# Hybrid layer on one core: the first chunk's keys are spread by VectorE out of PSUM, and the first scores follow at once

## The chip, the cores and the metric

The kernel runs on one core of a Trainium2 chip. The metric is the device time of one execution in microseconds (us). Times of engines and transfers come from one execution recorded by the hardware profiler. Engines are called PE (TensorE: matmuls, with PEld for its weight loads), DVE (VectorE), ACT (ScalarE), POOL (GpSimd) and SP (SyncE, which here only issues transfers).

## The reference

Input x is (4, 1024, 128) in float32. Four blocks follow each other, each added to x: a sparse causal attention with 16 heads of 8 channels, a feed-forward net with weights of +1 and -1, a Mamba block, and the same feed-forward net again. The change is in the attention, whose core is:

```python
x = x + attn(_layernorm(x), Wq, Wk, Wv, Wo)
# in attn: T = 1024, H = 16, HEAD_DIM = 8
mask   = causal & ((cols >= rows - 31) | ((rows - cols) % 64 == 0))
scores = einsum('bhqd,bhkd->bhqk', Q, K) * HEAD_DIM ** -0.5
attn   = softmax(where(mask, scores, -inf))
out    = einsum('bhqk,bhkd->bhqd', attn, V)
```

A query sees the 32 keys up to its own place, and every 64th key before.

## The kernel before

**Tiles and chunks.** A tile of the attention holds 64 places of two batch rows, 128 partitions in all. There are 32 tiles; four make a chunk (`cc`, 0 to 7). For each chunk `prep_steps` normalizes x (`xn`), turns it with PE (`tp`, copied by ACT as `xnT`), projects it to turned queries and keys (`pq`, `pk`, each a PSUM bank of 128 x 512) and to rows of queries, keys and values (`pn`, one per tile, from which ACT copies `qs`, `kv`, `vS`). The values also make a way through DRAM: a transfer `vd<-kv` writes them, four transfers `vr<-vd` read them in another order, and ACT spreads each of the four into `vb`.

**Keys.** The scores of near keys come from matmuls with 64 channels (8 heads) on the partitions at once. For that a chunk's keys stand in `kx`, 128 x (4 tiles x 8 x 128): for each partition, which belongs to one head, only the block of its own head holds keys, the other seven blocks are zero. There are two such buffers, `kxs`, cleared once by POOL (`gp.memset`). The keys get there by ACT's copy `kT<-pk` and 16 transfers `kx<-kT`, one per head. For chunk 0 they are dealt to the queues of SP, ACT and POOL, for chunk 1 to SP and POOL, later to SP alone.

**One tile.** `scores` (PE, into `ps`, one PSUM buffer for all tiles) and `keep_scores` (ACT copies the own half of ps to `S`), `scores_before` (DVE adds the masked other half by predicated copies), `softmax_scores` (DVE), `softmax_exp` (ACT, `E`). POOL forms the products for the strided keys (`prod`, `prodv`); PE turns the weights (`pt`), multiplies with `vb` (`pa`), and projects (`po`, `py`).

**Order.** Within the attention every instruction of PE, DVE, ACT and POOL keeps the order in which Python issues it (`InOrder`, whose line 57 therefore stands for nearly all instructions in the profile). Transfers issued by an engine stand in that engine's order too. The loop `for i in range(-LEAD, last + 5)` issues, in turn i, the stages of several tiles; `at(k, stage)` means the stage of tile i + k. A chunk's `prep_steps` is a generator that advances twice per turn; it starts in the turn that `starts` names, which is turn -7 for chunk 0, -6 for chunk 1 and 1 for chunk 2. The scores of tile i + 1 are issued in turn i, so those of tile 0 in turn -1, behind the preparation of chunk 1 so far issued. `spread_values` (ACT, one quarter of a chunk's values per turn) comes at the end of a turn, before the next turn's copy of S.

**The very start.** `tables` makes the identity, masks and small index tables from two POOL iotas (`row`, `col`). Behind it POOL clears kxs[0]; `stats` (DVE) and `scales` (POOL) of the first two chunks give the normalization; then POOL clears kxs[1] and both `vb`.

After the attention the feed-forward and Mamba parts run from queues of pieces whose order is fixed while the program is built.

Of the kernel before, what the change touches and what calls it, by code (L numbers as in the profile page):

```python
# [16 lines left out]
F32 = mybir.dt.float32  # L17
BF16 = mybir.dt.bfloat16
I32 = mybir.dt.int32
# [3 lines left out]
ALU = mybir.AluOpType  # L23
# [3 lines left out]
P = 128  # L27
# [4 lines left out]
H, HD = 16, 8  # L32
# [7 lines left out]
CH = 512  # L40
# [3 lines left out]
def hybrid_kernel(ctx: ExitStack, tc: tile.TileContext, x, Wq, Wk, Wv, Wo, ln_g, ln_b, W_in, conv_w,  # L44
                  conv_b, W_xp, W_dt, b_dt, A_log, D_param, W_out, res_scale, k0, k1, k2, s0, s1, s2, out):
    nc = tc.nc
# [15 lines left out]
    ve, te, sc, gp = (InOrder(e) for e in (nc.vector, nc.tensor, nc.scalar, nc.gpsimd))  # L62
    const = ctx.enter_context(tc.tile_pool(name="const", bufs=1))
# [32 lines left out]
    prev_mask = const.tile([P, W], I32, name="prev_mask")  # L96
    own_t = const.tile([P, W], F32, name="own_t")
    prev_t = const.tile([P, W], F32, name="prev_t")
    k0s = const.tile([P, 2, FF], U8, name="k0s")
    k1s = const.tile([P, 4, FF], U8, name="k1s")  # L100
    k2s = const.tile([P, 4, C], U8, name="k2s")
# [5 lines left out]
        for i, s in enumerate((s0, s1, s2, res_scale)):  # L107
            nc.sync.dma_start(scal[:, i : i + 1], s.partition_broadcast(P))

    def tables():  # L110
        with tc.tile_pool(name="setup", bufs=1) as setup:
            row = setup.tile([P, P], I32, name="row")
            gp.iota(row, pattern=[[0, P]], base=0, channel_multiplier=1)
            col = setup.tile([P, P], I32, name="col")
            gp.iota(col, pattern=[[1, P]], base=0, channel_multiplier=0)

            ve.tensor_tensor(ident, row, col, ALU.is_equal)
            row31 = row
            ve.tensor_single_scalar(row31, row, 31, op=ALU.bitwise_and)

            ve.tensor_tensor(prev_mask, col[:, :W], row31[:, :W], ALU.is_gt)

            ve.tensor_tensor(own_t, col[:, :W], row31[:, :W], ALU.is_ge)
            ve.tensor_tensor(prev_t, row31[:, :W], col[:, :W], ALU.is_gt)
            ve.tensor_copy(spread_ids[:, 0], row31[:, :N])
            ve.tensor_copy(spread_ids[:, 1], col[:, N : 2 * N])
# [64 lines left out]
    def attention(actx):  # L191
# [7 lines left out]
        pw = actx.enter_context(tc.tile_pool(name="attps", bufs=1, space=PSUM))  # L199
        pr = actx.enter_context(tc.tile_pool(name="attpr", bufs=5, space=PSUM))  # L200
        tiles = [(bp, m) for bp in range(NP) for m in range(NT)]
        HB = H // 2

        def spare(name):
            return pr.tile([P, CH], F32, tag="pr", name=name)
# [15 lines left out]
        sc.activation(warm, neg, AF.Exp)  # L221
        load_x(0, range(1, NT // 4), nc.sync)
        load_x(1, range(NT // 4), nc.sync)
        tables()

        def weights_in():
            wt = spare("wt")
# [23 lines left out]
            gp.tensor_scalar_mul(rs[:, 1], mv[:, :, 0], -1.0)  # L251
            gp.tensor_mul(rs[:, 1], rs[:, 1], rs[:, 0])

        gp.memset(kxs[0], 0.0)
        for cc in range(2):
            stats(cc)
            scales(cc)
        gp.memset(kxs[1], 0.0)
        for t in vbs:
            gp.memset(t, 0.0)  # L260
# [6 lines left out]
        prep = {}  # L267

        def prep_steps(cc):

            bp, c = divmod(cc, NT // 4)
            yield
            xn = ap2.tile([P, 4, C], F32, name=f"xn{cc}", tag="xn")
            rs = norms.pop(cc)
            for i in range(4):
                sc.activation(
                    xn[:, i, :], xs[bp][:, 4 * c + i, :], AF.Identity, bias=rs[:, 1, i : i + 1],
                    scale=rs[:, 0, i : i + 1],
                )
            yield  # L280
            tp = spare(f"tp{cc}")
            for i in range(4):
                te.transpose(tp[:, i * P : (i + 1) * P], xn[:, i, :], ident)
            yield
            xnT = ap2.tile([P, CH], F32, name=f"xnT{cc}", tag="xnT")
            sc.copy(xnT, tp)
            yield
            pq, pk = spare(f"pq{cc}"), spare(f"pk{cc}")
            te.matmul(pk, wqkv[:, 1, :], xnT, start=True, stop=True)
            te.matmul(pq, wqkv[:, 0, :], xnT, start=True, stop=True)  # L290

            def project(i):
                pn = spare(f"pn{cc}_{i}")
                te.matmul(
                    pn[:, : 3 * C], xnT[:, i * P : (i + 1) * P], wqkv.rearrange("p i c -> p (i c)"),
                    start=True, stop=True,
                )
                return pn

            qs = ap2.tile([P, 4, C], F32, name=f"qs{cc}", tag="qs")  # L300

            def keep_rows(i, pn):
                m = 4 * c + i
                sc.copy(qs[:, i], pn[:, :C])
                sc.copy(kv[bp][:, m], pn[:, C : 3 * C])
                sc.copy(vS[bp][:, :, m], pn[:, 2 * C : 3 * C])

            yield
            kT = ap2.tile([P, CH], F32, name=f"kT{cc}", tag="kT")
            sc.copy(kT, pk)  # L310
            kx = kxs[cc % 2]
            queues = ((nc.sync, nc.scalar, nc.gpsimd), (nc.sync, nc.gpsimd))[cc] if cc < 2 else (nc.sync,)
            for h in range(H):
                rows = slice(h * HD, (h + 1) * HD)
                queues[h % len(queues)].dma_start(
                    kx[rows, :, h % HB, :], kT[rows, :].rearrange("p (t x) -> p t x", t=4)
                )
            qT = ap2.tile([P, CH], F32, name=f"qT{cc}", tag="qT")
            sc.copy(qT, pq)
            for i0 in (0, 2):  # L320
                yield
                pn = project(i0), project(i0 + 1)
                yield
                keep_rows(i0, pn[0])
                keep_rows(i0 + 1, pn[1])
            vd = dram.tile([4, P, C], F32, name=f"vd{cc}")
            nc.sync.dma_start(vd.rearrange("t p c -> p t c"), kv[bp][:, 4 * c : 4 * c + 4, C:])
            vr = ap2.tile([P, 16, C], F32, name=f"vr{cc}", tag="vr")
            for a in range(4):
                nc.sync.dma_start(  # L330
                    vr[a * W : (a + 1) * W], vd.rearrange("t (g k) c -> k (t g) c", k=W)
                )
            prep[cc] = qT, kx, qs, vr
# [4 lines left out]
        def scores(i):  # L338

            bp, m = tiles[i]  # L340
            qT, kx, _, _ = prep[i // 4]
            q0 = i % 4 * P
            before_tile = prep[(i - 1) // 4][1][:, (i - 1) % 4] if m else None
            ps = psum["s", i] = pw.tile([P, H, 2, W], F32, name=f"ps{i}", tag="ps")
            for g in range(4):
                rows = slice(g * W, (g + 1) * W)
                for hf in range(2):
                    ch = slice(hf * 64, hf * 64 + 64)
                    heads = slice(hf * HB, (hf + 1) * HB)
                    q = qT[ch, q0 + g * W : q0 + (g + 1) * W]  # L350
                    te.matmul(
                        ps[rows, heads, 0, :], q, kx[ch, i % 4, :, g * W : (g + 1) * W], start=True, stop=True
                    )
                    if g % 2:
                        before = kx[ch, i % 4, :, (g - 1) * W : g * W]
                    elif m:
                        before = before_tile[ch, :, (g + 1) * W : (g + 2) * W]
                    else:
                        continue
                    te.matmul(ps[rows, heads, 1, :], q, before, start=True, stop=True)  # L360
            S[i] = ap2.tile([P, H, W + NT - 1], F32, name=f"S{i}", tag="S")

        def keep_scores(i):
            sc.copy(S[i][:, :, :W], psum["s", i][:, :, 0, :])
# [160 lines left out]

        LEAD = 7

        starts = {(cc if cc < 2 else 4 * cc) - LEAD: cc for cc in range(len(tiles) // 4)}
        preps = []
        last = len(tiles)  # L530
        for i in range(-LEAD, last + 5):
            def at(k, stage):
                if 0 <= i + k < last:
                    stage(i + k)

            if i == -LEAD:
                weights_in()
            if i == 0:
                load_mlp()
            at(-1, strided_products)  # L540
            at(1, product)
            at(-2, weights)
            at(0, scores_before)
            at(-4, divide)
            at(-2, strided)
            at(-2, weights_own)
            at(-2, weights_all)
            at(-2, weights_before)
            at(-5, project_out)
            at(-5, residual)  # L550
            at(1, scores)
            at(1, keep_scores)
            at(0, softmax_scores)
            at(0, softmax_exp)
            if i in starts:
                preps.append(prep_steps(starts[i]))
            for p in preps:
                next(p, None)
            at(-4, turn_out)
            at(-3, values)  # L560
            at(-4, keep_out)
            for p in preps:
                next(p, None)
            cc, step = divmod(i + LEAD, 4)
            if cc + 2 < last // 4:
                stats(cc + 2, range(step, step + 1))
                if step == 3:
                    scales(cc + 2)
            cc, step = divmod(i + 1, 4)
            if 0 <= cc < last // 4:  # L570
                spread_values(cc, range(step, step + 1))
# [681 lines left out]
```

## Time and profile before

| what | value |
|---|---|
| median of 3 runs | 932.8 us (928.43 to 935.38) |
| profiled execution, its own time | 934.96 us |
| its span | 933.2 us |
| mean granted PE clock | 0.89 |
| busy: PE, DVE, ACT, POOL | 760.7, 770.1, 589.3, 756.4 us |
| 0 to 27.7 us: busy PE, DVE, ACT, POOL | 16.5, 9.5, 13.2, 23.8 us |
| 60 to 90 us: busy PE, DVE, ACT, POOL | 24.2, 29.7, 20.4, 28.5 us of 30 |

The span is divided into busy time, per engine, and idle time, which the profile puts down to what ended it. A duration is that of one instruction or of a merged row of several (x4); rows can overlap a little, since an instruction begins while the one before it ends. "SPq", "ACTq" rows are transfers being issued, not their landing.

### The profile page before, as it was taken

Reading aid. Unit: us, or ns where it says so; the run is one execution under the profiler, and the core shown is the slowest. Engines: PE = TensorE matmul, PEld = TensorE weight load, DVE = VectorE, ACT = ScalarE, POOL = GpSimd, SP = SyncE. Lnnn points to the kernel's source line nnn. Section 1 sums busy time; section 2 is a strip of 40 time slices with the busy share of each in tenths; the row PEclk is TensorE's granted clock in tenths of the full one; section 3 lists DMA queues with packets and bytes.
Section 4 is the critical chain, followed back from the end, with each engine's and each line's share of the span. In section 5 each row is a group of like instructions: output and inputs, shape, how many; then the busy total and the mean of one; then the engine's idle time right before and its main releaser. Section 6 shows DMA issues by size and latency. Waiting matters only on the chain.

```text
span 933.2 us, 15285 instructions
## 1 busy us (share of the span) xinstructions
PE 760.7 (82%) x5628; PEld 457.0 (49%) x5628; DVE 770.1 (83%) x1026; ACT 589.3 (63%) x1293; POOL 756.4 (81%) x592
## 2 busy tenths in 40 slices
PE   5697758965697969887789889879889979788886
PEld 2355425643466634532347534536445626445556
DVE  4699898999743268988799999899999998999952
ACT  4676527753345578688666887777868764754613
POOL 8589996999533087999988999989989997997921
PEclk9799979997589989997898998989979988779988
DMA  5733123330100012111221121121211221222000
GB/s 131 128 69 70 26 50 68 71 68 2 30 18 1 27 65 69 46 68 47 67 70 45 51 85 47 67 69 46 79 70 46 79 81 46 80 67 80 24 22 12
DMA packets 47762, 53.35 MB, mean 57 GB/s; under 512 B 5032, under 2 KB 38960, under 8 KB 47688
## 3 DMA queue, kind: packets, MB, share of 16 engines
q1 hardware_dynamic: 46160, 51.69, 20.0%
q8 instruction: 44, 0.72, 0.3%
q0 software_dynamic: 768, 0.35, 0.3%
q10 hardware_dynamic: 760, 0.34, 0.2%
q14 instruction: 30, 0.25, 0.1%
HBM read 45.82 MB, written 4.46 MB: 54 GB/s over the span
## 4 chain that ended last, share of the span: by engine, by line
PE 22%; DVE 22%; ACT 13%; POOL 6%; issue 5%; DVEq 0%; POOLq 0%; ACTq 0%
DVE hs L57 14%; ACT da L57 4%; PE pys L57 4%; DVE hc L57 4%; ACT L57 3%; PE pc L57 3%; POOL db L57 3%; PE pga L57 3%; PE pgb L57 2%; POOL hc L57 2%; ACT waste L57 2%; PE pgc L57 1%; PE pmo L57 1%; PE pfob L57 1%; PE pmo_own L57 1%
## 5 line engine op out<-in xcount | busy, mean ns | idle before, releaser
L57 POOL TENSOR_TENSOR db<-du,bs 128x1024 f32<-128x1024 f32 x128 | 304.0, 2376 | 0.6 <-DMA bs<-bd 0.6
L57 ACT ACTIVATE da<-dt,a_t 128x512 f32<-128x512 f32 x256 | 175.5, 687 | 138.7 <-DVE hs L57 137.9
L57 POOL TENSOR_TENSOR hc<-hc,hc 128x512 f32<-128x512 f32 x128 | 163.8, 1281 | 48.5 <-DVE hc L57 48.4
L57 DVE TENSOR_TENSOR hc<-hs,pcc 128x1024 f32<-128x1024 f32 x128 | 155.9, 1218 | 20.3 <-PE pcc L57 12.2
L57 DVE TENSOR_TENSOR_SCAN hs<-da,db 128x512 f32<-128x512 f32 x128 | 149.1, 1206 | 13.7 <-ACT da L57 13.7
L57 DVE TENSOR_TENSOR_SCAN hs<-da,carry,db 128x512 f32<-128x512 f32 x128 | 157.0, 1268 | 1.9 <-ACT da L57 1.0
L57 PE MATMUL pys<-hc,ident 128*128 128x512 f32 x256 | 148.4, 666 | 0.1
L57 PE MATMUL pga<-h1a,w 128*128 128x512 f32 x256 | 76.3, 448 | 10.4 <-ACT u L57 2.9
L57 PE MATMUL pcc<-bc,spread 96*128 96x512 bf16 x128 | 52.1, 407 | 34.7 <-DVE hc L57 33.8
L57 PEld LDWEIGHTS pys<-hc,ident 128*128 128x128 f32 x256 | 52.0, 212 | 49.6 <-issue 24.8
L57 POOL TENSOR_TENSOR prodv<-vS,E 128x128 f32<-128x128 f32 (+14 forms) x30 | 69.5, 2318 | 6.7 <-ACT E L57 6.5
L57 POOL TENSOR_TENSOR prod<-kv,qs 128x128 f32<-128x128 f32 (+14 forms) x30 | 71.2, 2372 | 1.5 <-DVE or L57 1.4
L57 PEld LDWEIGHTS pga<-h1a,w 128*128 128x128 f32 x256 | 51.5, 206 | 34.7 <-issue 5.2
L57 ACT ACT_TABLE_LOAD x48 | 61.6, 1283 | 3.5 <-issue 2.7
L57 PE MATMUL pc<-mxnT,w_conv 128*128 128x512 f32 x128 | 62.1, 611 | 2.1 <-ACT gate L57 2.1
L57 PE MATMUL pgb<-h1b,w 128*128 128x512 f32 x192 | 59.3, 458 | 3.8 <-DVE h1b L57 2.7
L57 ACT ACTIVATE E<-S 128x512 f32<-128x512 f32 (+15 forms) x62 | 26.5, 473 | 52.5 <-DVE S L57 52.3
L57 PE MATMUL ps<-kx,qT 64*32 64x256 f32 x1008 | 46.4, 443 | 9.6 <-DVE S L57 9.4
L57 PE MATMUL py<-woT,oT 128*128 128x128 f32 x64 | 17.7, 362 | 41.1 <-ACT oT L57 40.9
L57 PEld LDWEIGHTS pgb<-h1b,w 128*128 128x128 f32 x192 | 39.2, 206 | 22.1 <-issue 6.4
L57 POOL TENSOR_TENSOR ep<-ep,eo 128x512 f32<-128x512 f32 x32 | 41.1, 1286 | 9.9 <-ACT ep L57 8.7
L57 POOL TENSOR_TENSOR du<-dt,u 128x512 f32<-128x512 f32 x16 | 20.8, 1304 | 27.9 <-ACT dt L57 27.9
(209 smaller groups left out, 1577.6 us busy)
## 6 DMA issues: line engine op xcount, KB each, us to landing
bs<-bd SPq DMA_DIRECT2D x64, 512.0 KB
vr<-vd SPq DMA_DIRECT2D x32, 256.0 KB
vd<-kv SPq DMA_DIRECT2D x8, 256.0 KB
x<-in_L_attn_a_x_dram SPq DMA_DIRECT2D x15, 128.0 KB
kx<-kT SPq DMA_DIRECT2D x110, 16.0 KB
out_dram<-x SPq DMA_DIRECT2D x12, 128.0 KB
taps<-in_L_attn_b_conv_w_dram SPq DMA_DIRECT2D x1, 512.0 KB
k1s<-in_L_ffn_k_dram SPq DMA_DIRECT2D x1, 256.0 KB
```

What stands on the lines that cost most here:

```text
L57: ins = getattr(self.engine, name)(*args, **kwargs)
```

## The change

Three things. First, chunk 0's keys no longer go through `kT` and transfers: four DVE operations, one per tile, multiply the bank `pk` (each key row repeated 8 times) with a small table `head_of`, 128 x 8, which is one where a block belongs to the partition's head and zero elsewhere; they write all of `kx`, so kxs[0] is no longer cleared. qT is copied first. Second, `tables` takes the statistics and scales of the first two chunks into itself, behind the identity and ahead of `head_of` and the other tables. Third, the scores of tile 0 and their copy are issued in turn -4, right behind the turn that spread the keys, and chunk 1's preparation starts in turn -4 instead of -6.

```diff
+    HB = H // 2
+    head_of = const.tile([P, HB], F32, name="head_of")
...
-    def tables():
+    def tables(stats, scales):
...
             ve.tensor_tensor(ident, row, col, ALU.is_equal)
+            for cc in range(2):
+                stats(cc)
+                scales(cc)
+
+            eight = setup.tile([P, HB], I32, name="eight")
+            ve.tensor_single_scalar(eight, row[:, :HB], 3, op=ALU.logical_shift_right)
+            ve.tensor_single_scalar(eight, eight, HB - 1, op=ALU.bitwise_and)
+            ve.tensor_tensor(head_of, eight, col[:, :HB], ALU.is_equal)
             row31 = row
...
-        tables()
...
-        gp.memset(kxs[0], 0.0)
-        for cc in range(2):
-            stats(cc)
-            scales(cc)
+        tables(stats, scales)
         gp.memset(kxs[1], 0.0)
...
             yield
-            kT = ap2.tile([P, CH], F32, name=f"kT{cc}", tag="kT")
-            sc.copy(kT, pk)
             kx = kxs[cc % 2]
-            queues = ((nc.sync, nc.scalar, nc.gpsimd), (nc.sync, nc.gpsimd))[cc] if cc < 2 else (nc.sync,)
-            for h in range(H):
-                rows = slice(h * HD, (h + 1) * HD)
-                queues[h % len(queues)].dma_start(
-                    kx[rows, :, h % HB, :], kT[rows, :].rearrange("p (t x) -> p t x", t=4)
-                )
             qT = ap2.tile([P, CH], F32, name=f"qT{cc}", tag="qT")
-            sc.copy(qT, pq)
+            if cc == 0:
+
+                sc.copy(qT, pq)
+                for t in range(4):
+                    ve.tensor_tensor(
+                        kx[:, t], pk[:, t * P : (t + 1) * P].unsqueeze(1).to_broadcast([P, HB, P]),
+                        head_of.unsqueeze(2).to_broadcast([P, HB, P]), ALU.mult,
+                    )
+            else:
+                kT = ap2.tile([P, CH], F32, name=f"kT{cc}", tag="kT")
+                sc.copy(kT, pk)
+                queues = (nc.sync, nc.gpsimd) if cc == 1 else (nc.sync,)
+                for h in range(H):
...
+                sc.copy(qT, pq)
+            prep[cc] = qT, kx
...
-        starts = {(cc if cc < 2 else 4 * cc) - LEAD: cc for cc in range(len(tiles) // 4)}
+        starts = {(3 if cc == 1 else 4 * cc) - LEAD: cc for cc in range(len(tiles) // 4)}
...
-            at(1, scores)
-            at(1, keep_scores)
+            if i == 3 - LEAD:
+                scores(0)
+                keep_scores(0)
+            if i >= 0:
+                at(1, scores)
+                at(1, keep_scores)
```

On SP the order of the first transfers changes with it: `vd` of chunk 0, then one key transfer of chunk 1, the four `vr` of chunk 0, the other seven key transfers of chunk 1, then `vd` and `vr` of chunk 1. Before, all of chunk 1's keys and both `vd` stood ahead of the `vr`.

More of the change, by code (lines that the diff above doesn't have):

```diff
@@ L201, in attention @@
         tiles = [(bp, m) for bp in range(NP) for m in range(NT)]
-        HB = H // 2
         def spare(name):
@@ L308, in prep_steps @@
             yield
-            kT = ap2.tile([P, CH], F32, name=f"kT{cc}", tag="kT")
-            sc.copy(kT, pk)
             kx = kxs[cc % 2]
-            queues = ((nc.sync, nc.scalar, nc.gpsimd), (nc.sync, nc.gpsimd))[cc] if cc < 2 else (nc.sync,)
-            for h in range(H):
-                rows = slice(h * HD, (h + 1) * HD)
-                queues[h % len(queues)].dma_start(
-                    kx[rows, :, h % HB, :], kT[rows, :].rearrange("p (t x) -> p t x", t=4)
-                )
-            qT = ap2.tile([P, CH], F32, name=f"qT{cc}", tag="qT")
-            sc.copy(qT, pq)
+            qT = ap2.tile([P, CH], F32, name=f"qT{cc}", tag="qT")
+            if cc == 0:
[10 more added lines that the diff above has]
+                for h in range(H):
+                    rows = slice(h * HD, (h + 1) * HD)
+                    queues[h % len(queues)].dma_start(
+                        kx[rows, :, h % HB, :], kT[rows, :].rearrange("p (t x) -> p t x", t=4)
+                    )
+                sc.copy(qT, pq)
+            prep[cc] = qT, kx
             for i0 in (0, 2):
@@ L340, in scores @@
             bp, m = tiles[i]
-            qT, kx, _, _ = prep[i // 4]
+            qT, kx = prep[i // 4][:2]
             q0 = i % 4 * P
```

## The prediction

> **What bounds the start now.** I read the page first (span, slices, groups), then the timeline of the first 36 us, since the change touches nothing later, and last the waits from 40 to 290 us. The page gives the span and the row that prices the new VectorE work.
>
> ```profile
> span 933.2 us, 15285 instructions
> ...
> L57 DVE TENSOR_TENSOR hc<-hs,pcc 128x1024 f32<-128x1024 f32 x128 | 155.9, 1218 | 20.3 <-PE pcc L57 12.2
> ```
>
> The timeline of the start (start, duration, engine, operation; in brackets the idle time before it and what ended it):
>
> ```profile
> 1.32 3.50 POOL L57 MEMSET kx<- 128x4096 f32 x1
> ...
> 1.73 3.18 DVE L57 TENSOR_SCALAR row<-row 128x128 int32<-128x128 int32 x1
> ...
> 5.41 0.29 DVE L57 BATCH_NORM_STATS2 sta<-x 128x6 f32<-128x128 f32 x1
> ...
> 9.18 1.65 ACT L57 ACTIVATE xn<-x,rsa 128x128 f32<-128x128 f32 x4 [2.48 <-POOL rsa L57]
> ...
> 12.03 2.07 PE L57 MATMUL pk<-xnT,wqkv 128*128 128x512 f32 x2 [0.68 <-ACT xnT L57]
> ...
> 19.09 0.59 ACT L57 COPY qT<-pq 128x512 f32<-128x512 f32 x1 [4.37 <-DMA kx<-kT]
> ...
> 22.97 5.82 SPq L315 DMA_DIRECT2D kx<-kT  x8
> 23.73 4.04 PE L57 MATMUL pn<-wqkv,xnT 128*128 128x384 f32 x12
> ...
> 27.70 1.11 PE L57 MATMUL ps<-kx,qT 64*32 64x256 f32 x24
> ...
> 29.55 0.82 DVE L57 COPY_PREDICATED_SCALAR S<-prev_mask,neg 32x512 f32 x1 [17.66 <-ACT S L57]
> ...
> 31.31 7.18 SPq L330 DMA_DIRECT2D vr<-vd  x8
> ...
> 34.68 0.62 ACT L57 COPY vb<-vr 32x512 f32<-32x512 f32 x1 [5.16 <-DMA vr<-vd]
> 35.21 0.58 ACT L57 COPY S<-ps 128x512 f32<-128x512 f32 x1
> ...
> 35.82 0.77 DVE L57 COPY_PREDICATED S<-prev_mask,ps 128x512 f32<-128x512 int32 x1 [1.19 <-ACT S L57]
> ```
>
> Four things are to be seen. VectorE's first table operation stands 3.18 us beside GpSimd's memset of kx and ends with it, and the statistics of x begin only behind it. ScalarE is held 4.37 us issuing key transfers before it may copy qT. The first scores (27.70) begin when TensorE's projections of both chunks end (23.73 + 4.04 = 27.77), so the arrival of the keys was not last there: order was. And tile 1's scores are copied at 35.21 because ScalarE stood 5.16 us in front of vb, waiting for the values' way through DRAM. VectorE, the engine that is nearly full afterwards, stands still for 17.66 us meanwhile. The waits from 40 to 290 us show what follows:
>
> ```profile
> ACT E L57 <- DVE S L57: 52.3, 26, 4.4
> PEld py L57 <- ACT oT L57: 48.3, 29, 4.0
> ```
>
> They are engine for engine, no transfer among them. So the attention behind tile 1 is a loop of engines that keeps its own pace, and what tile 1 gains the end gains. The mark I follow is VectorE's first operation on tile 1, at 35.82. In the built program the order of every engine's instructions from tile 3 on is the same before and after.
>
> **The change, part by part.** *Statistics first, no memset of the first kx.* The memset (3.50 us) and the table work are no longer ahead of the statistics, which now wait for x alone. The trace does not show when x's first quarter landed: at the latest at 4.74, when the weights queued behind it on ScalarE's queue released the first transpose; not before 3.3, when the DMA rates of the slices add up to its 262 KB. I take 4.1, so the statistics begin 1.3 us earlier (0.7 to 2.1). From there to pk's end the operations are those of before: four statistics pairs 1.7, GpSimd's scales 2.0, xn at 7.9, pk from 10.7 to 12.8, pq to 14.5.
>
> *Tables behind the statistics.* Three tiny operations are added (two on `eight`, one for `head_of`); the nearest rows, the copies of spread_ids at 5.25 and 5.33, follow each other at 0.1 us, so 0.3 to 0.5. The second chunk's x was there by 7.0, where its statistics began before; so its statistics end by 8.7, the tables and two pairs of the third chunk by about 10.5, and then VectorE waits for pk (12.8): free, with 2 us of cover. If GpSimd's scales held the tables for their longest operation (1.04 us), that would still be covered.
>
> *Spreading.* Four operations of 128x1024, one input in PSUM and one in SBUF. The row with the same output and the same kinds of input is hc<-hs,pcc, 1.22 us: 4 x 1.22 = 4.9 us, from 12.8 to 17.7. Only the first of them, done at 14.1, is waited for by the first scores; qT is later (pq 14.5, copy 0.59, 15.1). The four and five remaining statistics pairs (2.0 us) fall into the 17.66 us in which VectorE stood still. Without that cover they would cost 4.9.
>
> The row and the rule differ here. GpSimd clears the second kx and both vb from 10.7 on (8.7 and scales of 2.0): 3.5 + 2.0 + 1.0 + 2.0 + 1.0 = 9.5 us, to 20.2, just beside the spreading, and the row at 1.73 shows a VectorE operation standing until such a memset is over. The Trainium skill (SBUF — State Buffer, Who interferes with whom) says that only instructions in a two-port mode, or with two SBUF inputs against a GpSimd instruction that reads, share that lock; the integer operation on SBUF fits the first, a spread with one input in PSUM neither. By the row all four come after 20.2, the first scores at 21.4 instead of 15.1, and all behind them 6.3 us later, a net loss of 1.0; by the rule nothing. I take the rule, as the trace has statistics operations (0.26 us at 11.42) unhindered beside the second memset, though they have a single source.
>
> *Removed.* kT's copy of chunk 0 (0.58), five issues on ScalarE (the 4.37 us), six on SP, five on GpSimd. No data wait goes with them on TensorE, as shown; they free the queues.
>
> *First scores at once, chunk 1 two turns later.* Now the way to 35.82 in the new order. Scores of tile 0 at 15.1; rows of ps give 1.11 for 24 at 27.70 and twice as long in slow places, I take 1.5: 16.6. Then S's copy 0.6 (17.25), and the projections of chunk 0, 1.65 for each two (16.45 in the timeline): 18.3 and 19.9. ScalarE: two tiles' rows 1.3 (to 18.95), xn of chunk 1 1.65 (20.6), two more tiles 1.3 (21.9), xnT 0.6 (22.5). TensorE: pk of chunk 1 2.07 (24.6; 1.13 elsewhere, which would bring 0.9 more). kT 0.6 (25.25). SP now has vd of chunk 0, one key transfer, then the four vr, then the other seven. So vr, whose data left at 21.9 and landed by 24.3, waits behind the one that needs kT: 0.7 us, vr issued at 25.95. From issue to vb's start it was 34.68 - 31.31 = 3.37: 29.3. ScalarE is there at 28.4 (behind pk 1.8 for pq, 4 x 0.34 for two projections, 0.65 for the last copies), so vr decides by 0.9. vb 0.62, S of tile 1 0.6: **VectorE begins tile 1 at 30.55, against 35.82: 5.3 us earlier.**
>
> VectorE's work on tile 0 runs meanwhile: spreading and statistics to 19.7, then 4.7 us (29.55 to 34.2 before): 24.4, and tile 1's scores, which reuse its bank, come at 27.9 by TensorE's order. Slack 3.5 us: the spread could cost 0.9 more each and take nothing.
>
> *Who else comes late.* Queued behind GpSimd's eight key issues, which wait for kT (25.25), is prod of tile 1: 8 x 0.54 = 4.3, so 29.6 to 30.1, in time by a hair; 1 us late would cost at most that. On SP the seven keys go behind vr, by 0.7 to 0.8 each and with waits on vr's landings: last issue about 32, landed by 35.5; tile 4's scores need them at 44.43 - 5.3 = 39.1. Cover 3.6 us. vd and vr of chunk 1 follow, landing from about 38.5; needed at 48.94 - 5.3 = 43.6.
>
> Sum: 5.3 us, 4.7 to 7.0 by the bounds of x's landing and pk. The profiled execution took 934.96 (span 933.2 and 1.8 around it), which becomes 929.7; it lay 2.2 above the median, and on the median 932.8 - 5.3 = **927.5**.
>
> **The rivals.** *Larger gain.* vr lands before ScalarE is there, pk and the scores run at their quick rows: another 0.9 + 0.9 + 0.4, x at 3.3 adds 0.8: 8.3, 924.5, and with a favourable draw of the runs' scatter below 923.5. For it: the quick rows exist; against: vr's 3.37 stood on a nearly empty queue. *Nothing gained.* Either the memsets hold the spreads (the row at 1.73; loss 1.0), or vr shares its engines with the keys issued by GpSimd and takes twice 3.37 to vb: gain 1.9. 931 to 934. For it: that the transfer engines were 0.80 busy from 27.7 to 36 us already. *Slower.* The key transfers on SP behind vr run one after the other, each waiting for the landing of one before, at 3.4 us: seven give 24 from 29.5, so 53 at tile 4's scores. It decides once the last key lands after 44.4, the place of those scores before; at 53 it would be 8.6 us slower, 941.4. Against it: eight such transfers took 5.82 at 22.97, 0.73 each.
>
> **How the numbers follow.** Forecast 0.64, larger gain 0.14, nothing gained 0.17, slower 0.05. The three runs of before spread from 928.43 to 935.38, so a median of after can be 3 off by scatter alone. The range goes from 922 (the larger gain with some scatter) to 933.5 (most of nothing gained). Some 1%, 9.3 us, is about what a measurement of this kernel can tell from no change; faster than 923.5 are half of the larger gains and a little of the forecast's scatter, 0.10; slower than 942.1 half of the last and a trace, 0.03; within, 0.87.
>
> **What would show it.** In the profile of after: statistics from about 4.1; four spreads of 1.2 us at 12.8; ps at 15; VectorE's first predicated copies of tile 0 near 20; vb's wait on vr ending at 29.3; tile 1 on VectorE at 30.5, and ps of tile 4 not waiting for keys; further on the same rows 5 us earlier. It would be wrong if a spread takes 2 us or more, if kT of chunk 1 comes after 26, or if a wait on kx stands before tile 4.

## The result, and the profile after

Twelve executions of each kernel, taken side by side, gave a median of 928.91 us after (924.76 to 930.8) against 932.62 before (928.12 to 935.38): the ratio is 0.9962, with a 95% interval from 0.994 to 0.9984, which is 1.5 to 5.6 us faster. A second comparison, of 17 executions after with 34 before, gave 926.48 against 932.58, a ratio of 0.9941 (0.9926 to 0.9956). The forecast was 927.5, a gain of 5.3; the two medians found 3.7 and 6.1. Before's executions lie in two groups, 22 of the 99 on record at 927.9 to 929.2 us and the others at 931.0 to 935.4, while after's 29 lie at 924.8 to 931.1, so that the medians compare mixtures and after's two are 0.7 slower and 1.8 faster than the middle of before's first group.

The profiled execution of after took 928.12 us, its span on the page is

```profile
span 926.3 us, 15255 instructions
```

The timeline of its start answers to the one shown of before (start, duration, engine, operation; in brackets the idle time before it and what ended that):

```profile
4.46 0.29 DVE L57 BATCH_NORM_STATS2 sta<-x 128x6 f32<-128x128 f32 x1 [2.76 <-DMA x<-in_L_attn_a_x_dram]
...
8.25 1.65 ACT L57 ACTIVATE xn<-x,rsa 128x128 f32<-128x128 f32 x4 [1.55 <-POOL rsa L57]
...
8.80 0.22 DVE L57 TENSOR_SCALAR row<-row 128x128 int32<-128x128 int32 x1
...
10.44 3.51 POOL L57 MEMSET kx<- 128x4096 f32 x1
...
13.21 4.62 DVE L57 TENSOR_TENSOR kx<-pk,head_of 128x1024 f32<-128x1024 f32 x4 [2.73 <-PE pk L57]
...
13.89 6.09 POOL L57 MEMSET vb<- 128x2304 f32 x10
14.59 0.59 ACT L57 COPY qT<-pq 128x512 f32<-128x512 f32 x1 [3.54 <-PE pq L57]
...
15.23 1.12 PE L57 MATMUL ps<-kx,qT 64*32 64x256 f32 x24 [0.68 <-ACT qT L57]
...
16.28 2.85 PE L57 MATMUL pn<-wqkv,xnT 128*128 128x384 f32 x8
...
19.82 0.78 DVE L57 COPY_PREDICATED_SCALAR S<-prev_mask,neg 32x512 f32 x1
...
24.75 1.95 SPq L345 DMA_DIRECT2D vr<-vd  x4
...
28.74 0.62 ACT L57 COPY vb<-vr 32x512 f32<-32x512 f32 x1 [2.62 <-DMA vr<-vd]
...
29.88 0.78 DVE L57 COPY_PREDICATED S<-prev_mask,ps 128x512 f32<-128x512 int32 x1 [4.99 <-ACT S L57]
```

VectorE's table operation, 3.18 us beside the memset before, takes 0.22; the statistics wait for x alone. The four spreads take 1.155 us each although GpSimd clears kx and both vb beside them all the time. ScalarE copies qT at 14.59 instead of 19.09, the first scores begin at 15.23 instead of 27.70, and VectorE starts tile 1 at 29.88 instead of 35.82: 5.94 us earlier. ScalarE still stands in front of vb, 2.62 us instead of 5.16.

From there the shift stays. The reduction of tile 10 to its maximum comes 6.35 us earlier than before, that of tile 31 6.2 us earlier, and the span ends 6.9 earlier. The waits from 40 to 290 us are the same as before to within 1 us (who waited for whom: us in all, times, longest):

```profile
ACT E L57 <- DVE S L57: 52.2, 26, 4.5
PEld py L57 <- ACT oT L57: 47.4, 29, 4.0
```

So between these two profiles the gain was made in the first 30 us and kept. What is left to explain is which of the three edits brought it, and whether the covers that the prediction named (idle time of an engine in which added work costs nothing) were really there.

### The profile page after: what moved, and what is told of

Same layout as the page of the kernel before. It is cut to its first block, busy times and chain, and to the rows that moved or that the text cites. A ratio compares the mean times of both kernels' runs of the same rounds, so it can differ in the third digit from the quotient of the medians.

```text
span 926.3 us, 15255 instructions
## 1 busy us (share of the span) xinstructions
PE 753.8 (81%) x5628; PEld 454.6 (49%) x5628; DVE 772.2 (83%) x1033; ACT 588.9 (64%) x1292; POOL 751.3 (81%) x586
## 3 DMA queue, kind: packets, MB, share of 16 engines
HBM read 45.82 MB, written 4.46 MB: 54 GB/s over the span
## 4 chain that ended last, share of the span: by engine, by line
DVE 33%; PE 25%; ACT 16%; POOL 12%; issue 8%; SPq 3%; DMA 3%; DVEq 0%; POOLq 0%; ACTq 0%
DVE hs L57 16%; DVE hc L57 5%; ACT da L57 4%; PE pys L57 4%; PE pga L57 4%; POOL prod L57 3%; DVE S L57 3%; POOL prodv L57 3%; ACT L57 3%; PE pc L57 3%; SPq L330 2%; PE pfoa L57 2%; POOL db L57 2%; PE pd L57 2%; PE pgb L57 2%
## 5 line engine op out<-in xcount | busy, mean ns | idle before, releaser
L57 PE MATMUL pys<-hc,ident 128*128 128x512 f32 x256 | 144.5, 650 | 0.1
L57 PE MATMUL pgb<-h1b,w 128*128 128x512 f32 x192 | 56.9, 443 | 5.0 <-DVE h1b L57 3.9
L57 ACT COPY ep<-pt 128x512 f32<-128x512 f32 x32 | 18.8, 587 | 38.5 <-DVE eo L57 36.6
```

The costliest lines, as they stand in the source:

```text
L57: ins = getattr(self.engine, name)(*args, **kwargs)
```

## The experiments

The mark in all of them, the point whose shift is followed, is the start of VectorE's first full-width predicated copy of tile 1: 35.82 before, 29.88 after.

**Statistics first alone.** The kernel before, with only the statistics and scales moved into `tables`; the memset of the first kx stays, in front of them on GpSimd.

```diff
-    def tables():
+    def tables(stats, scales, clear):
...
+            clear()
+            for cc in range(2):
+                stats(cc)
+                scales(cc)
```

> The kernel before with one edit: the statistics of the first two chunks stand ahead of the tables, behind the identity; the first kx is still cleared, keys still go by transfers, scores and chunks in the old order. Mark: VectorE's first predicated copy of tile 1 (before 35.82, after 29.88 us). My theory, that the gain is one of order and the early statistics are a part of it: statistics at about 4.5, xn at 8.3, mark about 0.9 earlier, 34.9. Rival, that the start is hidden behind the transfers of keys and values: mark unchanged at 35.8.

```profile
4.58 0.29 DVE L57 BATCH_NORM_STATS2 sta<-x 128x6 f32<-128x128 f32 x1 [2.88 <-DMA x<-in_L_attn_a_x_dram]
...
8.47 0.19 DVE L57 TENSOR_SCALAR row<-row 128x128 int32<-128x128 int32 x1
...
13.94 5.20 ACTq L315 DMA_DIRECT2D kx<-kT  x5
...
19.18 0.59 ACT L57 COPY qT<-pq 128x512 f32<-128x512 f32 x1 [5.27 <-DMA kx<-kT]
...
20.31 1.13 PE L57 MATMUL pk<-xnT,wqkv 128*128 128x512 f32 x2 [3.53 <-ACT xnT L57]
...
35.09 0.77 DVE L57 COPY_PREDICATED S<-prev_mask,ps 128x512 f32<-128x512 int32 x1 [2.04 <-ACT S L57]
```

This is its timeline. The same two rows of before, the issues on ScalarE's queue and pk of chunk 1:

```profile
14.75 4.29 ACTq L315 DMA_DIRECT2D kx<-kT  x5
...
20.22 2.07 PE L57 MATMUL pk<-xnT,wqkv 128*128 128x512 f32 x2 [2.11 <-ACT xnT L57]
```

The statistics come 0.83 us earlier than in before (5.41), and xn 0.81 earlier (8.37). There the gain ends: ScalarE's five issues took 5.20 us here against 4.29 (why stays open), and qT is copied at 19.18, even 0.09 later than before. The mark still moves by 0.73, within 0.2 us of what the theory had, but that is luck. It comes from TensorE, whose pk of chunk 1 took 1.13 us here and 2.07 in the profile of before: kT follows 0.86 earlier (21.47 against 22.33), and so do SP's transfers up to vr (30.45 against 31.31). By itself, moving the statistics gave nothing at the mark. One execution took 928.69, but that says nothing of the edit. At tile 31 it was 1.41 us ahead of the profile of before and at the end 6.3, with the same instructions in between.

**Only the memset put back.** After, with the memset of kxs[0] again behind the iotas.

```diff
+            clear()
             for cc in range(2):
                 stats(cc)
                 scales(cc)
...
-        tables(stats, scales)
+        tables(stats, scales, lambda: gp.memset(kxs[0], 0.0))
```

> The changed kernel with the memset of the first kx put back in its old place on GpSimd (behind the two iotas). My theory, that only the two-port table operation suffers from the memset and has been moved out of its way: statistics at 4.5, mark 29.9 as after. Rival, that the memset on GpSimd itself was in the way: scales and xn 0.9 later, mark 30.8.

Measured: memset at 1.32 for 3.50 us, mark at 30.28. That lies between the theory and the rival, and the steps in front of it decide: the statistics begin at 4.55 and xn at 8.34, each 0.09 behind after, so the memset holds up next to nothing. The other 0.3 us come in with TensorE's pq (1.91 us against 1.59), which lets ScalarE begin qT only at 15.01 instead of 14.59. Here the memset did no harm, with the integer table operation no longer beside it.

**Only the tables put back in front of the statistics**, without the memset.

```diff
-            for cc in range(2):
-                stats(cc)
-                scales(cc)
-
             eight = setup.tile([P, HB], I32, name="eight")
...
+            for cc in range(2):
+                stats(cc)
+                scales(cc)
```

> The changed kernel with the tables ahead of the statistics as before, but without the memset of the first kx. My theory: the table operation then takes 0.2 us instead of 3.18 and all tables are done before x lands, so statistics at 4.5 and mark 29.9 as after. Rival, that the order of tables and statistics counts by itself: statistics at 5.4, mark 30.8.

```profile
2.10 0.22 DVE L57 TENSOR_SCALAR row<-row 128x128 int32<-128x128 int32 x1
...
4.37 0.29 DVE L57 BATCH_NORM_STATS2 sta<-x 128x6 f32<-128x128 f32 x1 [1.45 <-DMA x<-in_L_attn_a_x_dram]
```

The table operation takes 0.22, the statistics wait for x alone, and xn begins at 8.14. So the tables in front cost nothing either; only both together made the 3.18 us. The mark itself is 31.99, 2.1 later than in after. It is not the tables: tile 0's scores took 1.99 us here for 24 matmuls against 1.12, and the eight pn behind them 4.25 against 2.85, which put chunk 1 back.

**The old order with the spread.** After, with chunk 1 started in turn -6 again and tile 0's scores issued in turn -1.

```diff
-        starts = {(3 if cc == 1 else 4 * cc) - LEAD: cc for cc in range(len(tiles) // 4)}
+        starts = {(cc if cc < 2 else 4 * cc) - LEAD: cc for cc in range(len(tiles) // 4)}
...
-            if i == 3 - LEAD:
-                scores(0)
-                keep_scores(0)
-            if i >= 0:
-                at(1, scores)
-                at(1, keep_scores)
+            at(1, scores)
+            at(1, keep_scores)
```

> The changed kernel with the old order: chunk 1 prepared from turn -6, scores of tile 0 in turn -1; keys of chunk 0 spread by VectorE, statistics first. My theory, that the order brings about half of the gain: first scores at about 25, vr again behind both vd, vb's wait ends at about 31.7, mark about 32.9, so 2.9 earlier than before, and the time 2 to 4 us above that of the changed kernel. Rival, that spreading instead of transfers brings it all: mark 29.9, time as the changed kernel.

```profile
14.62 0.59 ACT L57 COPY qT<-pq 128x512 f32<-128x512 f32 x1 [2.09 <-PE pq L57]
...
21.83 1.11 PE L57 MATMUL ps<-kx,qT 64*32 64x256 f32 x24
...
30.32 0.62 ACT L57 COPY vb<-vr 32x512 f32<-32x512 f32 x1 [6.66 <-DMA vr<-vd]
...
31.45 0.76 DVE L57 COPY_PREDICATED S<-prev_mask,ps 128x512 f32<-128x512 int32 x1 [2.69 <-ACT S L57]
```

The mark is at 31.45, between the theory's 32.9 and the rival's 29.9. Tile 0's scores come 5.87 us earlier than before in the *old* order. Some 4.1 us of this come because ScalarE, no longer held by issues, copies qT 4.47 us earlier, so that pk of chunk 1 begins at 16.15 instead of 20.22. The other 1.8 are TensorE's: pk and pq of chunk 1 took 1.02 us each here, 2.07 and 1.81 in the profile of before. What stays behind is the way of the values: vr again stands behind all of chunk 1's keys on SP (issued at 26.70 instead of 24.75), and ScalarE waits 6.66 us for it. So 4.37 of after's 5.94 us appear without the new order, some 0.7 of them as in the first experiment by the short rows of chunk 1. The median was 927.65 (924.98 to 931.69, 20 executions), ratio 0.9952 (0.9935 to 0.9969), between the two medians of after: the 2 to 4 us that had been expected above it did not show.

**After once more**, for its second median and a second profile.

> The changed kernel again, nothing edited. Open: the profile of it has the attention 6.3 us earlier, the medians say 3.7. My theory, that the start itself differs between executions by TensorE's clock (keys and projections of both chunks at the rows 1.12 or 2.07), and that the first profile was a quick one: the mark (29.88 in the first profile) comes 0.5 to 2 us later, at 30.4 to 32, and the median stays 3 to 5 below that of before. Rival, that the attention always ends 6.3 earlier and the work behind it loses 2.6: mark again 29.9 within 0.2, last tile again at 229.1.

```profile
15.42 1.99 PE L57 MATMUL ps<-kx,qT 64*32 64x256 f32 x24 [0.68 <-ACT qT L57]
...
17.33 4.28 PE L57 MATMUL pn<-wqkv,xnT 128*128 128x384 f32 x8
...
30.63 0.62 ACT L57 COPY vb<-vr 32x512 f32<-32x512 f32 x1 [2.10 <-DMA vr<-vd]
...
31.77 0.78 DVE L57 COPY_PREDICATED S<-prev_mask,ps 128x512 f32<-128x512 int32 x1 [6.99 <-ACT S L57]
```

The same kernel has its mark at 31.77 here, 1.9 us later than in the first profile, as expected; that the cause is TensorE's clock, as the theory had it, is not shown (last section). Tile 0's scores begin within 0.2 us of the first profile (15.42 against 15.23) and then take 1.99 against 1.12, the eight pn 4.28 against 2.85: 2.3 us, which are there again at vr's issue (27.17 against 24.75). The median of 926.48 is 6.1 below before; 3 to 5 had been expected.

**The values ahead of all keys on SP.** After, with SP's transfers kept in the order they are issued in Python, so that chunk 0's vr no longer wait behind one key transfer of chunk 1.

```diff
+    sy = InOrder(nc.sync)
...
-                queues = (nc.sync, nc.gpsimd) if cc == 1 else (nc.sync,)
+                queues = (sy, nc.gpsimd) if cc == 1 else (nc.sync,)
...
+            down = sy if cc < 2 else nc.sync
```

> The changed kernel with the four vr of chunk 0 ahead of all keys of chunk 1 on SP. My theory, that vr sets the mark and that it stood behind the key transfer that waits for kT: vr issued at 23.7 instead of 24.75, vb's wait ends at 27.7, mark 28.8, about 1.1 earlier, and the keys of chunk 1 still land before tile 4's scores; time 1 us less. Rival, that vr takes its time from the share of the transfer engines, not from its place: mark 29.9, or the keys late at tile 4 and the time above that of the changed kernel.

```profile
22.38 2.07 PE L57 MATMUL pk<-xnT,wqkv 128*128 128x512 f32 x2 [1.45 <-ACT xnT L57]
...
23.96 1.92 SPq L57 DMA_DIRECT2D vr<-vd  x4
...
27.97 0.63 ACT L57 COPY vb<-vr 32x512 f32<-32x512 f32 x1
...
29.21 0.78 DVE L57 COPY_PREDICATED S<-prev_mask,ps 128x512 f32<-128x512 int32 x1 [4.21 <-ACT S L57]
```

ScalarE waits no longer for the values (vb at 27.97 has no wait), so the prediction's "vr decides by 0.9" was right in kind, and with vr off the path the mark is 0.7 earlier than in the profile of after. That is although pk of chunk 1 took 2.07 us here instead of 1.12; in after, where vr stands behind kT, such a pk would have put the mark at about 30.8 (an estimate from these rows), so at equal rows the edit is worth about 1.6. GpSimd's products for tile 1 now start at 30.02, and VectorE waits 0.54 us for them. Median 927.02 (922.44 to 930.34, 10 executions), ratio 0.9948 (0.992 to 0.9977), between the two of after: the 1 us less that had been expected is not resolved.

**The spread done twice.** Eight spread operations instead of four, tiles 0, 1, 2, 3 and again, with the same values.

```diff
-                for t in range(4):
+                for t in (0, 1, 2, 3, 0, 1, 2, 3):
```

> The changed kernel with each of the four spreading operations made twice, eight in all, the same values. My theory, that the spread has 3.5 us of cover before tile 1's scores: 4.6 us more on VectorE, its work on tile 0 ends at 29.1 instead of 24.5, scores of tile 1 then wait for it and the mark comes at about 31, 1.1 to 1.3 later. Rival, that the spread lies on the path: mark 4.6 later, 34.5; second rival, that all is covered: 29.9.

```profile
13.01 9.14 DVE L57 TENSOR_TENSOR kx<-pk,head_of 128x1024 f32<-128x1024 f32 x8 [2.69 <-PE pk L57]
...
18.90 1.99 PE L57 MATMUL ps<-kx,qT 64*32 64x256 f32 x24 [4.30 <-DVE kx L57]
...
36.14 0.78 DVE L57 COPY_PREDICATED S<-prev_mask,ps 128x512 f32<-128x512 int32 x1 [6.91 <-ACT S L57]
```

The mark fell at 36.14, later than any of the expectations, and 4.4 later than in the profile of after with the same 1.99 us scores. The wait names why: the scores of tile 0 waited 4.30 us for the fifth operation, which writes tile 0's keys again. My edit had moved the first scores by 3.5 us (15.42 to 18.90), and these passed on in full; the rest is pk of chunk 1, 1.93 us here against 1.12. The median went to 932.88, ratio 1.0008 (0.9988 to 1.0029): the whole gain was gone. The run shows what the first scores are worth (its other cost, the work behind them, is small by the next run), not whether the spread is covered.

**The spread lengthened behind its first operation.** The same, with the four additional operations on tiles 1, 2, 3 and 1.

```diff
-                for t in range(4):
+                for t in (0, 1, 2, 3, 1, 2, 3, 1):
```

> After with four more spread operations (the four tiles, then tiles 1, 2, 3, 1 again), so that the first scores still wait for the first one alone and VectorE has 4.6 us more work in front of tile 0's chain. Theory (the spread is covered, by 3.5 us behind tile 0 as the prediction had it): first scores where they were (15.2 to 15.5), tile 0's masked copies begin at 24.4 instead of 19.8, the scores of tile 1 follow them at 27.6 instead of 25.2, VectorE begins tile 1 at 30.0 to 30.5 in an execution with TensorE's quick rows at the start (ps x24 1.1, after: 29.88) or 31.8 to 32.3 with its slow ones (ps x24 2.0, 31.77). Behind that up to 1.1 us more, since GpSimd's scales, its key issues and tile 1's products come 2 us later. Rival (no cover, all of it passes on): 34.5 or 36.4. Median within 1.5 of after for the theory, 4 to 5 slower for the rival.

```profile
13.09 9.14 DVE L57 TENSOR_TENSOR kx<-pk,head_of 128x1024 f32<-128x1024 f32 x8 [2.76 <-PE pk L57]
...
15.09 1.12 PE L57 MATMUL ps<-kx,qT 64*32 64x256 f32 x24 [0.68 <-ACT qT L57]
...
24.22 0.79 DVE L57 COPY_PREDICATED_SCALAR S<-prev_mask,neg 32x512 f32 x1
...
27.44 2.01 PE L57 MATMUL ps<-kx,qT 64*32 64x256 f32 x32 [2.35 <-DVE S L57]
...
30.15 0.77 DVE L57 COPY_PREDICATED S<-prev_mask,ps 128x512 f32<-128x512 int32 x1 [0.89 <-ACT S L57]
```

Here the cover is seen at work: 4.52 us more of VectorE move tile 0's masked copies from 19.82 to 24.22 and tile 1's scores, which need the bank, from 25.16 to 27.44; the mark moves by 0.27, and that with tile 1's 32 matmuls taking 2.01 us instead of 1.14. VectorE's idle time in front of tile 1 shrinks from 4.99 to 0.89 us. The maximum of tile 1 comes 0.43 later than in after, because GpSimd's products are late too. The median was 929.27 (925.36 to 932.09, 20 executions), ratio 0.9968 (0.9955 to 0.9981), against 0.9962 and 0.9941 of after: 0.4 us above the first median of after and 2.8 above the second, so the cover is shown by the marks and not settled by the medians.

**A version with the rest of the wait taken out.** The values first on SP as above, and ScalarE's copies into vb of chunk 0 one turn later, so that tile 1's copy of S does not stand behind the first of them; six of chunk 1's keys on GpSimd instead of eight.

```diff
-                    queues[h % len(queues)].dma_start(
+                    queues[int(cc == 1 and h % 8 in (1, 4, 6))].dma_start(
...
-                spread_values(cc, range(step, step + 1))
+                part = range(step, step + 1) if cc else ((), (0,), (1,), (2, 3))[step]
+                spread_values(cc, part)
```

> The one above with vr first, and besides ScalarE's four vb copies of chunk 0 each a turn later (the last two together), and six instead of eight of chunk 1's key transfers on GpSimd, ten on SP. My theory, that vb in front of S is what holds tile 1: S of tile 1 follows its scores at 26.4, mark at 27.0, 2.9 earlier than the changed kernel, and the time 2 to 3 us less than it. Rival, that something else is 1 to 2 us behind (prod of tile 1 on GpSimd, keys of chunk 1 on SP at tile 4): tile 5 no more than 1 us earlier than in the changed kernel.

Measured: mark at 28.95 although ps was the long one (1.99 for 24), 2.8 below the 31.77 of after with the same ps (0.6 of it because the eight pn took 3.61 here against 4.28), but short of the 27.0 expected. TensorE gives tile 1's scores only at 28.1, since the projections of chunk 1 stand in front of them. Median 924.53, from six executions, so it was run again:

> The kernel of e8 once more, to see whether its 924.5 holds. If moving the first vb copies out of the way of tile 1's copy is worth what the traces show (2.8 us at tile 1 in executions of the same TensorE rows, 1.5 to 2.3 at tile 31): median 924 to 925.5, 1 to 3 us below after. If it was the draw of few runs: 926 to 928.

```profile
28.67 0.59 ACT L57 COPY S<-ps 128x512 f32<-128x512 f32 x1 [0.36 <-PE ps L57]
29.30 0.78 DVE L57 COPY_PREDICATED S<-prev_mask,ps 128x512 f32<-128x512 int32 x1 [4.42 <-ACT S L57]
```

924.87 us (921.55 to 927.41, 9 executions), ratio 0.9923 (0.99 to 0.9947); the first time 0.9926 (0.9898 to 0.9954). In the timeline ScalarE's copy of tile 1 waits for TensorE's scores alone, no longer for a transfer. Both medians lie below both of after, by 1.6 to 4.4 us, and against the executions of before that they were taken with they gain 8.1 and 8.6, where the change gained 3.7 and 6.1. The intervals of the ratios overlap at their ends, so that it beats after is likely by two medians and by the marks, and no more than that. Which of its three edits counts was not tried apart.

## Why the prediction was right

**The statistics.** Foreseen at 4.1, they began at 4.46 in after, and between 4.27 and 4.58 in the other runs: x lands later than the middle I took between 3.3 and 4.74. The gain at xn was 0.93 instead of 1.3. The first and the third experiment show that it came from parting the table work from the memset, and that either half would have done. That it went on to the first scores took the other edit: in the first experiment, with the key issues still on ScalarE, it was lost before qT.

**The spread.** 4.62 us for four against 4.9, with three memsets beside them the whole time. The rule of the Trainium skill (SBUF — State Buffer, Who interferes with whom) held in this case, and the row of 3.18, which would have given 21.4 for the first scores, did not apply: the integer operation on SBUF was held, the operation on a PSUM bank with a small SBUF table was not. What such a delay would have cost is now priced as well: 3.5 us on the first scores took the whole gain of the median away.

**The cover.** The slack behind tile 0 was put at 3.5 us. The run with 4.52 us more behind the first operation let 0.27 through, with first scores 0.14 earlier than in after and matmuls of tile 1 that took 0.87 longer, so the slack was about 4 us (an estimate from these rows). It holds for what stands behind the first operation alone: in front of the first scores there is none.

**The way to tile 1**, term by term (predicted, profile of after): first scores 15.1, 15.23; their 24 matmuls 1.5, 1.12; eight pn 3.3, 2.85; pk of chunk 1 2.07, 1.12; kT 24.6, 23.12; vr issued 25.95, 24.75; from issue to vb 3.37, 3.99; mark 30.55, 29.88. The sum was right because its errors had both signs: TensorE's rows were 1.8 us shorter in this execution, vr 0.6 longer. In the second profile TensorE had 1.99, 4.28 and 1.12, vr took 3.46, and the mark was 31.77. The gain of 5.3 at the mark lies between the two profiles' 5.94 and 4.05. Nor is all of 5.94 the change's: the profile of before had the long pk of chunk 1 (2.07), and the first experiment, whose qT was as late as before's, had its mark at 35.09 with the short one. At like rows the gain is 5.2, so close to 5.3 by luck as well. Why vr took 3.4 to 4.0 us in the profiles stays open; that GpSimd's key transfers share engines with it was only argued.

**What was put down to the wrong edit.** The prediction wrote of the removed transfers that "no data wait goes with them on TensorE", they "free the queues", since TensorE's order and not the keys' arrival released the first scores. That was true of the last step and too narrow for the path to it. TensorE's projections of chunk 1 were themselves late because ScalarE had stood 4.37 us behind its own key issues. With that gone, pk of chunk 1 begins 4.07 us earlier in the old order. By the marks of executions with short rows, moving the statistics alone is worth nothing, the spread with the statistics 3.6 (35.09 to 31.45), and the new order on top 1.6 (31.45 to 29.88); its effect on the median was not resolved. No run has the spread with late statistics. The 0.93 us at xn are there again at pk of chunk 0, on the path to the first scores, so that share of the 3.6 is argued, not shown.

**The late comers.** Tile 1's products start at 28.67 (29.6 to 30.1 foreseen) and are there when VectorE asks at 30.54. SP's last key goes out at 32.6, and tile 4's scores, at 38.13, waited 0.21 us for GpSimd's `ep`, not for keys. The slower rival, with keys running one behind the other at 3.4 us, did not come: seven took 5.85.

**The end.** What tile 1 had gained, 5.94, was still there at tile 31, 6.2. In all twelve profiles tile 31's maximum comes 198.1 to 200.4 us behind the mark, so what the start gains or loses does reach it. From there to the end of the span the same instructions took 697.9 us in the profile of before and 693.0 to 698.1 in the others, whatever the start: the first experiment, with its late mark, ended at 928.69 by a rest of 693.0, and the run with the values ahead, by a rest of 693.2 behind an early mark, at 922.64. That puts a scatter of up to 5 us on any single time, and it fits that the medians of one and the same kernel found 3.7 and 6.1. It also leaves something open: no profile of before from its group at 928 us was taken, so whether that group has the late start with a short rest, and how much of the gain of the medians is the start alone, is not shown. The prediction's allowance of 3 us for scatter was about right.

## What to carry to other kernels

When an engine's order, and not data, releases an instruction, ask next what made that order late: here it was a copy standing behind the issue of transfers on its own queue. Work put on a busy engine is free where a timeline shows it standing still, but only behind the operation that others wait for: 4.5 us added behind the first spread cost 0.3 at the mark, 3.5 us in front of the first scores cost the whole gain of the median. Where several terms meet close to each other, taking out the last one gives only the distance to the next: without the values' wait tile 1 came 0.7 us earlier (about 1.6 at equal rows), since ScalarE's copies and TensorE's projections were next. And a mark that lands where the theory had it proves nothing until the steps in front of it are followed: in the first experiment the 0.7 that seemed to confirm it came from another engine.

## What the runs showed of the hardware

TensorE's matmuls at the start differed between executions of the same kernel: the first 24 score matmuls took 1.12 or 1.99 us, the eight pn behind them 2.85 or 4.28, with starts within 0.2 us of each other. The stretch from 15 to 18 us, first in the first profile of after, then in the second (busy time of PE, PEld, DVE, ACT and POOL, then the granted clock, the transfer engines' share and GB/s):

```profile
15.00:18.00 3.00, 2.77 (x30) 1.60 (x31) 3.00 (x4) 1.54 (x6) 2.77 (x6) 1.00 0.31 51
...
15.00:18.00 3.00, 2.58 (x25) 1.22 (x26) 2.96 (x5) 0.85 (x2) 2.77 (x6) 1.00 0.23 29
```

The granted clock is 1.00 in both, as it is from 13 to 22 us. The Trainium skill (TensorE: Matmul & The Clock Gate, What's actually happening) has a window that runs free of the kernel, so that the moment at which a kernel gets the full rate differs from run to run. The ratio of 1.99 to 1.12 is near the factor of two between that gate's rates, but the clock row of this profile does not show it, so that cause is not shown here. What is shown is the price: 1.9 us at tile 1 in the same kernel, more than the 1.6 of the new order.

An integer operation on SBUF (128 x 128) took 3.18 us beside a memset of GpSimd and 0.19 to 0.22 away from it, while operations with their large input in PSUM took 1.155 us each beside memsets of 3.5 and 6.1 us. The two differ in kind and in type of operand as well as in the place of their input, and no run here tells these apart.
